# Pinv's transpositions moved into the slots, the first attn3 placed beside projections, and the first input in four parts behind products of constants

## The chip, the cores and the metric

The kernel runs on one core of a Trainium2 chip, in fp32. Its engines are TensorE (PE, with its weight loads PEld), VectorE (DVE), ScalarE (ACT), GpSimd (POOL) and SyncE (SP, which only issues DMAs here). The metric is the device time of one execution in microseconds (us). Each engine works through its own list of instructions in order; semaphores make one engine wait for another.

## The reference, cut to what matters

The input x has the shape 2 x 512 x 64 x 32: two images, 512 channels, 2048 tokens each. Two layers follow one another.

```python
# layer 0: softmax attention, 8 heads of 64
q, k = [x, emb] @ Wq, [x, emb] @ Wk ;  v = x @ Wv
x = x + softmax(q k^T / 8) v @ Wout + bout
# layer 1: Nystroem attention on LN(t), then a linear map on LN(t)
q, k, v = split(LN(t) @ Wqkv) ;  q = q * 64**-0.5
qL, kL = means of q, k over 8 tokens                 # 256 landmarks
attn1 = softmax(q kL^T) ; attn2 = softmax(qL kL^T) ; attn3 = softmax(qL k^T)
z = attn2^T / (max(col sums) * max(row sums))
for 6 iterations:  xz = attn2 z ; z = z (13 I - xz (15 I - xz (7 I - xz))) / 4
out = attn1 (z (attn3 v)) + depthwise convolution of v over 33 tokens
t = t + out @ Wout + bout
t = t + (LN(t) @ dequant(qidx, scales)^T) @ W^T
```

`pinv` below is the iteration. The scale of z contains a maximum over all images and heads, so no iteration starts before attn2 of all of them is known.

## The kernel before, in words

Channels or head dimensions lie on the 128 partitions. The eight heads of an image are worked on as four **pairs**, two heads of 64 rows in the two halves of the partitions; with two images there are eight pairs. Tokens are cut in four blocks of 512 (NTB = 4) or sixteen of 128 (NST = 16), the 512 channels in four parts of 128 (KC = 4).

**Order.** Engines PE, DVE, ACT and POOL carry out instructions in the order in which the program records them. The program is therefore a set of Python generators: each `yield` closes a unit of work, and the driving code takes units from several generators in turn, so that one's TensorE work stands between another's dependent steps. SP's queue of DMAs is ordered by the framework.

**Layer 0.** Class `Heads0` projects a pair's q, k and v; `attention0` computes scores, exponentials and products. At the start, the embedding of the frequency and time positions (`embedded`, L858 to L869) is a small product fp on TensorE, a copy ft on DVE, and an addition e_q over 128 x 2048 on POOL; `project` (L874 to L877) multiplies one 512 token block of x by a 128-column slice of Wq, and DVE adds e. The first x block is loaded by one DMA of 1 MB (L825).

**Layer 1, first part.** Class `Pair` has the parts as methods. `keys_and_queries` projects k and q and makes landmarks (L1209, label pp). `attend` makes attn2 of both heads, called X, in a tile of the single-buffered tags M0/M1 or Q0/Q1 by turns; `gram` makes the product X^T X, A; `front` is both. `others` runs the projections of an image's second to fourth pair with the front of the pair before beside them. `start_scale` forms the common scale zs from the sums of all eight pairs; its maximum over partitions is taken on POOL.

**Layer 1, main loop.** `todo` is the list of the eight pairs, the second image's first. Round n runs `pinv` for pair n. The iteration keeps, per head h, a 256 x 256 symmetric matrix and 64 more columns in the tiles M[h] and R[h]; only the upper blocks are computed, and `flip` (L1493 to L1497) supplies the lower left one: TensorE transposes a 128 x 128 block into PSUM (tp_M, tp_R), ScalarE copies it back. An iteration is: product pa of M with itself for both heads, DVE writes R and M from it (`less`, L1520); product pb of R with itself, DVE writes M. The head-0 flip of M is called before a product, the others inside one, between its first and second pass over the contraction (`between`). After the iterations three steps form u from M (wp on TensorE, a copy, tp, `less`).

Between these dependent products `pinv` calls `slot`, seventeen times a round: twice in each of five iterations, once before the last, and twice in each of the three u steps. One slot takes a unit of each of three lists: `before`, the attn1 of the previous pair (16 units: scores and exponentials twice, av with a DVE addition, row sums rs with a reciprocal and a multiplication on DVE and an addition into o on POOL, four times over); `nexts`, the `second` of the next pair (four value projections vp, nine steps of attn3, the landmark values, the convolution of v by a banded matrix, the start value y0 by the product wp_y, an ACT copy called wide, and the transposition tp_y); and, from round 5, `finish`, the output projection and last stage of the second image. In odd slots below ten a second unit of `before` follows.

The attn3 of a pair (`attn3`) has a step's scores on TensorE, the exponential p on ACT, an addition into acc3 (tags Q0/Q1) on DVE, and in the next step the product av on TensorE. The first pair has no round before it: its `second` ran beside the last pair's `front`, which takes one unit of it at its one place, and the rest then ran alone, followed by `start_scale` in between.

**The last stage.** Class `Finish1` works on a 512-token block g of the first image: the residual, then LayerNorm in steps (`statistics`: two additions on DVE, L952 and L953; mean by a product with the constant matrix mean_w on TensorE, L956; subtraction; squares; variance; root; reciprocal L1626) and the combined map of both weights (`map_units`, fp_g, L1656). The string in the driving code takes single units: 1 is attn1 of the last pair, f finish, a and b output projections of blocks 0 and 1, s a LayerNorm step of block 0.

PSUM has three sorts of banks in layer 1: `bank` (three in rotation), `product_bank` (two) and `side_bank(n)` (single ones; flips use 0, attn1's av 1, attn3's av 3).

Of the kernel before, what the change touches and what calls it, by code (L numbers as in the profile page):

```python
# [10 lines left out]
F32 = mybir.dt.float32  # L11
# [650 lines left out]
def fast_path(  # L662
# [159 lines left out]
            tiles.append(xb)  # L822
        return tiles

    xbs = load_x(x, 0, "x0", 0, 1)  # L825
    load_w0("k", slice(0, P))
    xbs += load_x(x, 0, "x0", 1, NTB - 1)
    wv_sb = wpool0.tile([P, KC, C], F32, name="wv_f")
# [349 lines left out]
    class Pair:  # L1178
# [59 lines left out]
        def attend(self):  # L1238

            i, L = self.i, self.L  # L1240
            kind = "MQ"[i % 2]
            X = self.X = [
                zpool.tile([P, 2, LM + 1], F32, tag=f"{kind}{h}", name=f"X_{i}_{h}") for h in range(2)
            ]
            rs = small.tile([P, 4], F32, tag="rs2", name=f"rs2_{i}")
            for h in range(2):
                nc.gpsimd.memset(X[h][:, :, LM:], 1.0)
            for h in range(2):
                rows_h = slice(h * D, (h + 1) * D)
                sc = bank(f"sc2_{i}_{h}")  # L1250
                for t in range(2):
                    nc.tensor.matmul(
                        sc[:, t * LM : (t + 1) * LM],
                        lhsT=L[0][rows_h, t * P : (t + 1) * P],
                        rhs=L[1][rows_h, :],
                        start=True,
                        stop=True,
                    )
                nc.scalar.activation(X[h][:, :, :LM], sc.rearrange("p (t n) -> p t n", n=LM), AF.Exp)  # L1259
            for h in range(2):  # L1260
                two = slice(2 * h, 2 * h + 2)
                x_h = X[h][:, :, :LM]
                nc.vector.tensor_reduce(rs[:, two], x_h, AX.X, ALU.add)
                nc.vector.reciprocal(rs[:, two], rs[:, two])
                nc.vector.tensor_tensor(
                    x_h, x_h, rs[:, two].unsqueeze(2).to_broadcast([P, 2, LM]), ALU.mult
                )
                nc.sync.dma_start(X_d[self.b, self.hp, h], x_h)
                nc.vector.tensor_reduce(rsum[:, i, two], x_h, AX.X, ALU.add)
# [229 lines left out]
        def pinv(self, slot):  # L1499
# [32 lines left out]
            for it in range(PINV_ITERS - 1):  # L1532
                for h in range(2):
                    pr = square(M[h], f"pa_{it}_{h}_{self.name}", flip)
                    less_in_blocks(R[h], 3.5 * CUBE, M[h], pr)
                    less_in_blocks(M[h], 3.25 / rest, M[h], pr)
                    flip = R[h], f"R{h}_{it}"
                slot()
                for h in range(2):
                    pr = square(R[h], f"pb_{it}_{h}_{self.name}", flip)  # L1540
                    less_in_blocks(M[h], rest, M[h], pr)
                    flip = None
                slot()
                self.flip(M[0], f"M0_{it}")
                flip = M[1], f"M1_{it}"
            slot()
            self.flip(*flip)

            self.u = lmpool.tile([P, 2, P], F32, tag="u", name=f"u_{self.name}")
            src = [M[h][:, :, LM:] for h in range(2)]  # L1550
# [262 lines left out]
    next(units)  # L1813
    drain(beside(pairs[0][-1].front(), units))
    drain(units)
    drain(others(1, xhs, pairs[1][0]))

    todo = pairs[1] + pairs[0]

    def second(n):  # L1820

        pair = todo[n]
        yield from pair.values(xhs_of[n // NPAIR])
        if n == NPAIR - 1:
            xhs_of.append(load_x(xh_d, 0, "xh2"))
        yield from pair.attn3()
        landmarks = pair.landmarks_values()
        next(landmarks)
        yield

        if n <= NPAIR:
            o = qopool.tile([P, S], F32, tag="qo", name=f"o_{pair.name}")
        else:
            o = None if n < len(todo) - 1 else late_buffer(f"o_{pair.name}")
        convolution = pair.convolution(o)
        next(convolution)
        yield
        next(landmarks)
        yield
        next(convolution)  # L1840
        yield
        drain(convolution)
        yield from pair.start_values()

    def late_buffer(name):

        return block_of(xpool, "xb", name).rearrange("p k n -> p (k n)")

    xhs_of = [xhs]
    todo[0].prefetch()  # L1850
    v = second(0)
    next(v)
    drain(beside(pairs[1][-1].front(), v))
    start_scale()
    drain(v)


    before, nexts, finish, made = [], [], [], 0

    def slot():  # L1860

        nonlocal made
        i = made % 17
        made += 1
        advance(before)
        advance(nexts)
        if i < 10 and i % 2:
            advance(before)
        advance(finish)

    todo[0].prefetch1(kvpool.tile([P, S], F32, tag="k", name="q2_first"))
    for n, pair in enumerate(todo):
        if n + 1 < len(todo):
            todo[n + 1].prefetch()
            nexts.append(second(n + 1))
        if n == NPAIR + 2:
# [43 lines left out]

    st = [f.steps(deviation_of(t)) for t, f in enumerate(fs)]

    for c in "1f1f1f1f11f1f1a1a1a1as1bs1s1b1b1b":
        if c == "f":
            advance(finish)
        else:
            next({"1": before[0], "a": outs[0], "b": outs[1], "s": st[0]}[c])
    assert not finish
    drain(before[0])
    drain(outs[1])  # L1930
# [12 lines left out]
    for t in range(NTB):  # L1943
        maps = fs[t].map_units(wide_banks)
        if t + 1 < NTB:
            next(st[t + 1])
            turns(maps, None, st[t + 1], None, st[t + 1], None, None, st[t + 1])
        else:
            drain(maps)
# [91 lines left out]
```

## Time and profile before

| | us |
|---|---|
| Three runs | 2883.84, 2885.5, 2886.38 |
| Median | 2885.5 |
| Profiled execution, its time | 2885.05 |
| Its span, first to last instruction | 2883.1 |
| TensorE busy | 2783.7 (97%) |
| VectorE busy | 1779.4 (62%) |
| ScalarE busy | 920.7 (32%) |
| GpSimd busy | 224.7 (8%) |
| TensorE's mean granted clock | 0.991 |
| Longest wait of PE at a flip (tp_M) | 6.0 |
| DVE reciprocal of 128 x 512, each (32 of L1599) | 3.35 |

A profile is one execution recorded by the hardware. A line of the timeline gives the start and duration in us, the engine, the line in the kernel, the operation, output and inputs by name, the shape, how many instructions are drawn together, and in brackets the idle time before it and what ended that. The waits view sums such idle time by the waiting and the releasing line: total us, times, longest. The windows view gives for a stretch each engine's busy time with the number of instructions, then the granted TensorE clock (1.00 full, 0.50 half), the DMA share and GB/s. An "issue" entry is a time in which an engine waited for nothing that the profile shows.

### The profile page before, as it was taken

The numbers are of one execution on the slowest core, as the hardware profiler recorded it, in microseconds if no ns is written. First come the engines' busy times: TensorE is split into PE (matmuls) and PEld (weight loads), VectorE is DVE, ScalarE is ACT, GpSimd is POOL, SyncE is SP. The second block draws the span as 40 slices with busy tenths as digits, with TensorE's granted clock in tenths as the row PEclk, the third lists the DMA queues.
The fourth block names the chain that finished last, engine by engine and source line by source line (L and its number), as shares of the span: only waits on it lengthen the run. The fifth ranks groups of instructions, "written<-read, shape, count | busy, mean of one in ns | idle before, by whom it ended". The sixth has DMA issues, their size and how long they took to land. (4 is left out here: it accounts for less than half of the span.)

```text
span 2883.1 us, 39570 instructions
## 1 busy us (share of the span) xinstructions
PE 2783.7 (97%) x16706; PEld 1365.1 (47%) x16706; DVE 1779.4 (62%) x2133; ACT 920.7 (32%) x1352; POOL 224.7 (8%) x130
## 2 busy tenths in 40 slices
PE   8999999999999999999999999999999999898899
PEld 4343443434443334343344456656666665554334
DVE  3869788765667766667666543464554555555565
ACT  1344434433243344344222222222322323222210
POOL 1101011010102110100011000000000000000000
PEclk9999999999999999999999999999999999999999
DMA  3000000101012000020145441102100102020201
GB/s 114 1 5 1 5 1 1 60 15 45 26 45 88 30 1 1 1 87 15 45 165 185 162 149 43 32 28 87 49 28 25 63 1 105 1 73 8 95 12 49
DMA packets 85578, 140.31 MB, mean 49 GB/s; under 512 B 7808, under 2 KB 42896, under 8 KB 82832
## 3 DMA queue, kind: packets, MB, share of 16 engines
q1 hardware_dynamic: 80896, 120.87, 12.6%
q0 software_dynamic: 4416, 16.79, 1.5%
q8 instruction: 133, 2.18, 0.3%
q14 instruction: 53, 0.43, 0.0%
q10 hardware_dynamic: 80, 0.03, 0.0%
HBM read 82.48 MB, written 55.19 MB: 48 GB/s over the span
## 5 line engine op out<-in xcount | busy, mean ns | idle before, releaser
L1053 DVE TENSOR_TENSOR acc_f<-acc_f,p_f 128x1024 f32<-128x1024 f32 x448 | 611.4, 1365 | 216.5 <-ACT p_f L1043 187.4
L1043 ACT ACTIVATE p_f<-sc_f 128x1024 f32<-128x1024 f32 x512 | 496.7, 1022 | 578.5 <-PE sc_f L1035 572.4
L1035 PE MATMUL sc_f<-q_f,k_f 64*64 64x512 f32 x4096 | 491.7, 595 | 2.9 <-ACT p_f L1043 2.9
L1065 PE MATMUL av_f<-p_f,v_f 64*64 64x512 f32 x4096 | 484.3, 589 | 0.0
L1065 PEld LDWEIGHTS av_f<-p_f,v_f 64*64 64x64 f32 x4096 | 156.5, 133 | 283.1 <-issue 283.1
L1035 PEld LDWEIGHTS sc_f<-q_f,k_f 64*64 64x64 f32 x4096 | 144.7, 133 | 293.9 <-issue 253.1
L1209 PE MATMUL pp<-xh,w 128*128 128x512 f32 x512 | 229.0, 602 | 4.2 <-ACT X L1259 3.5
L1506 PE MATMUL pa<-M 128*128 128x192 f32 (+1 forms) x640 | 157.2, 384 | 0.1
L1209 PEld LDWEIGHTS pp<-xh,w 128*128 128x128 f32 x512 | 96.5, 192 | 127.7 <-issue 115.6
L1506 PE MATMUL pb<-R 128*128 128x192 f32 (+1 forms) x640 | 152.2, 384 | 2.2 <-ACT R L1497 2.2
L1599 DVE RECIPROCAL rinv<-rinv 128x512 f32<-128x512 f32 x32 | 107.3, 3352 | 52.7 <-ACT rinv L1598 46.9
L1084 POOL TENSOR_TENSOR q_f<-q_f,rinv_f 128x512 f32<-128x512 f32 x32 | 68.3, 2135 | 825.6 <-DVE rinv_f L1083 825.5
L919 PEld LDWEIGHTS vp<-w,xh 128*128 128x128 f32 x1024 | 120.0, 196 | 21.6 <-issue 16.3
L1601 POOL TENSOR_TENSOR o<-o,rinv 128x512 f32<-128x512 f32 x32 | 46.9, 1466 | 1007.1 <-DVE rinv L1600 969.2
L919 PE MATMUL vp<-w,xh 128*128 128x128 f32 x1024 | 125.0, 282 | 0.0
L1506 PEld LDWEIGHTS pb<-R 128*128 128x128 f32 x640 | 107.3, 190 | 32.4 <-issue 10.6
L919 PEld LDWEIGHTS vp_f<-wv_f,x 128*128 128x128 f32 x1024 | 115.6, 192 | 12.7 <-issue 11.0
L1520 DVE SCALAR_TENSOR_TENSOR R<-M,pa 128x320 f32<-128x320 f32 (+1 forms) x160 | 60.0, 416 | 98.2 <-PE pa L1506 97.2
L1520 DVE SCALAR_TENSOR_TENSOR M<-M,pb 128x320 f32<-128x320 f32 (+1 forms) x160 | 59.3, 416 | 99.3 <-PE pb L1506 97.7
L874 PE MATMUL pp_q_f<-x,wq_f 128*128 128x512 f32 x256 | 118.0, 614 | 1.8 <-DVE q_f L877 0.7
L919 PE MATMUL vp_f<-wv_f,x 128*128 128x128 f32 x1024 | 118.5, 276 | 0.0
L934 PE MATMUL yp_f<-q_f,wo_f 128*128 128x512 f32 x256 | 114.2, 599 | 4.3 <-DVE rinv_f L1083 3.3
(192 smaller groups left out, 3153.8 us busy)
## 6 DMA issues: line engine op xcount, KB each, us to landing
xh<-xh_fd SPq DMA_DIRECT2D x12, 1024.0 KB, 5.1
x<-in_x_dram SPq DMA_DIRECT2D x8, 1024.0 KB, 5.3
xr_f<-in_x_dram SPq DMA_DIRECT2D x8, 1024.0 KB, 5.1
x_fd<-xr_f POOLq DMA_DIRECT2D x8, 1024.0 KB, 4.6
xh_fd<-xn_f POOLq DMA_DIRECT2D x8, 1024.0 KB, 4.6
k_fd<-k SPq DMA_DIRECT2D x32, 256.0 KB, 2.6
q_fd<-q SPq DMA_DIRECT2D x32, 256.0 KB, 2.8
xb_g<-x_fd SPq DMA_DIRECT2D x32, 256.0 KB, 4.7
```

The source lines that it names most:

```text
L874: nc.tensor.matmul(pp, lhsT=w_sb[kind][:, k, cols], rhs=xbs[t][:, k, :], start=k == 0, stop=k == KC - 1)
L919: nc.tensor.matmul(vp[:, j * P : (j + 1) * P], lhsT=xb[:, k, j * P : (j + 1) * P], rhs=w_of(k), start=k == 0, stop=k == KC - 1,)
L934: nc.tensor.matmul(yp, lhsT=wo_sb[:, k, m * P : (m + 1) * P], rhs=oTs[k][:, toks], start=k == 0, stop=k == NPAIR - 1,)
L1035: nc.tensor.matmul(sc[r * D : (r + 1) * D, h, :], lhsT=hd.k[rows, lo : lo + D], rhs=hd.q[rows, t * TB : (t + 1) * TB], start=True, stop=True,)
L1043: nc.scalar.activation(p, sc, AF.Exp, scale=D**-0.5)
L1053: nc.vector.tensor_tensor(acc, first if c == 1 else acc, p, ALU.add)
L1065: nc.tensor.matmul(av[r][half, :], lhsT=hd.v[keys, c, half], rhs=pp[keys, h, :], start=c == 0, stop=c == NST - 1,)
L1084: nc.gpsimd.tensor_tensor(o, o, rinv, ALU.mult)
L1209: nc.tensor.matmul(pp, lhsT=self.w[j][:, c, :], rhs=xhs[t][:, c, :], start=c == 0, stop=c == KC - 1)
L1506: nc.tensor.matmul(dst, lhsT=lhsT[:, k, t * P : (t + 1) * P], rhs=rhs[:, k, :], start=k == 0, stop=k == 1)
L1520: nc.vector.scalar_tensor_tensor(out, m, scale, pr, ALU.mult, ALU.subtract)
L1599: nc.vector.reciprocal(rinv, rinv)
```

## The change

- **The first input.** The DMA of the first x block is cut in four, one for each 128 channels. Twenty products of the constant mean_w with itself are put into an otherwise unused bank ahead of the first product on TensorE.
- **Tags of X.** `attend` always uses the tags M0/M1, no longer Q0/Q1 in turn.
- **Flips.** In `pinv`, the flip of R[0] leaves the inside of the product pa of head 1 and goes into the following slot; the flip of M[0] leaves its place just before the next product and goes into the slot before it; so does the last flip of M[1]. `slot` takes a function `between` for this and calls it after the first unit of `before`, ahead of `nexts`. The flips of R[1] and M[1] stay inside products.
- **Two units in slot 0.** The first slot of each round takes two units of `nexts` instead of one.
- **y0.** In `second`, the product wp_y comes before the convolution's second half, and tp_y after it; before, both came after.
- **The first pair's attn3.** `second(0)` is taken one unit at a time beside the projections of the second image's later pairs (`others(1, ...)`), from the eleventh unit on. The next pair's prefetch and value projections stand around the last pair's `front` and `start_scale`, before round 0, so round 0's slots have fewer units of `nexts` left.
- **The end.** A "t" at the end of the string takes the first LayerNorm step of block 1 (the two DVE additions) ahead of block 0's reciprocal; the loop then doesn't take it a second time.

```diff
@@ -822,7 +822,12 @@
             tiles.append(xb)
         return tiles
 
-    xbs = load_x(x, 0, "x0", 0, 1)
+    xbs = [block_of(xpool, "xb", "x0_0_0")]
+    for k in range(KC):
+        nc.sync.dma_start(xbs[0][:, k, :], chunked(x[0])[:, k, :TB])
+    warm = bank("warm")
+    for i in range(20):
+        nc.tensor.matmul(warm[:, :P], lhsT=mean_w, rhs=mean_w, start=True, stop=True)
     load_w0("k", slice(0, P))
     xbs += load_x(x, 0, "x0", 1, NTB - 1)
     wv_sb = wpool0.tile([P, KC, C], F32, name="wv_f")
@@ -1238,10 +1243,7 @@
         def attend(self):
 
             i, L = self.i, self.L
-            kind = "MQ"[i % 2]
-            X = self.X = [
-                zpool.tile([P, 2, LM + 1], F32, tag=f"{kind}{h}", name=f"X_{i}_{h}") for h in range(2)
-            ]
+            X = self.X = [zpool.tile([P, 2, LM + 1], F32, tag=f"M{h}", name=f"X_{i}_{h}") for h in range(2)]
             rs = small.tile([P, 4], F32, tag="rs2", name=f"rs2_{i}")
             for h in range(2):
                 nc.gpsimd.memset(X[h][:, :, LM:], 1.0)
@@ -1534,17 +1536,16 @@
                     pr = square(M[h], f"pa_{it}_{h}_{self.name}", flip)
                     less_in_blocks(R[h], 3.5 * CUBE, M[h], pr)
                     less_in_blocks(M[h], 3.25 / rest, M[h], pr)
-                    flip = R[h], f"R{h}_{it}"
-                slot()
+                    flip = None
+                slot(lambda: self.flip(R[0], f"R0_{it}"))
+                flip = R[1], f"R1_{it}"
                 for h in range(2):
                     pr = square(R[h], f"pb_{it}_{h}_{self.name}", flip)
                     less_in_blocks(M[h], rest, M[h], pr)
                     flip = None
-                slot()
-                self.flip(M[0], f"M0_{it}")
+                slot(lambda: self.flip(M[0], f"M0_{it}"))
                 flip = M[1], f"M1_{it}"
-            slot()
-            self.flip(*flip)
+            slot(lambda: self.flip(*flip))
 
             self.u = lmpool.tile([P, 2, P], F32, tag="u", name=f"u_{self.name}")
             src = [M[h][:, :, LM:] for h in range(2)]
@@ -1813,8 +1814,6 @@
     next(units)
     drain(beside(pairs[0][-1].front(), units))
     drain(units)
-    drain(others(1, xhs, pairs[1][0]))
-
     todo = pairs[1] + pairs[0]
 
     def second(n):
@@ -1837,40 +1836,54 @@
         yield
         next(landmarks)
         yield
+        start = pair.start_values()
+        next(start)
+        yield
         next(convolution)
         yield
         drain(convolution)
-        yield from pair.start_values()
+        next(start)
+        yield
 
     def late_buffer(name):
 
         return block_of(xpool, "xb", name).rearrange("p k n -> p (k n)")
 
+
     xhs_of = [xhs]
-    todo[0].prefetch()
-    v = second(0)
-    next(v)
-    drain(beside(pairs[1][-1].front(), v))
+    first = second(0)
+    for i, _ in enumerate(others(1, xhs, todo[0])):
+        if i == 8:
+            todo[0].prefetch()
+        if i >= 10:
+            next(first, None)
+    drain(first)
+    todo[1].prefetch()
+    nexts = [second(1)]
+    advance(nexts)
+    for n in todo[NPAIR - 1].front():
+        advance(nexts, n // 2)
     start_scale()
-    drain(v)
-
-
-    before, nexts, finish, made = [], [], [], 0
-
-    def slot():
+    advance(nexts)
+
+
+    before, finish, made = [], [], 0
+
+    def slot(between=lambda: None):
 
         nonlocal made
         i = made % 17
         made += 1
         advance(before)
-        advance(nexts)
+        between()
+        advance(nexts, 2 if i == 0 else 1)
         if i < 10 and i % 2:
             advance(before)
         advance(finish)
 
     todo[0].prefetch1(kvpool.tile([P, S], F32, tag="k", name="q2_first"))
     for n, pair in enumerate(todo):
-        if n + 1 < len(todo):
+        if n and n + 1 < len(todo):
             todo[n + 1].prefetch()
             nexts.append(second(n + 1))
         if n == NPAIR + 2:
@@ -1920,11 +1933,11 @@
 
     st = [f.steps(deviation_of(t)) for t, f in enumerate(fs)]
 
-    for c in "1f1f1f1f11f1f1a1a1a1as1bs1s1b1b1b":
+    for c in "1f1f1f1f11f1f1a1a1a1as1bs1s1b1b1bt":
         if c == "f":
             advance(finish)
         else:
-            next({"1": before[0], "a": outs[0], "b": outs[1], "s": st[0]}[c])
+            next({"1": before[0], "a": outs[0], "b": outs[1], "s": st[0], "t": st[1]}[c])
     assert not finish
     drain(before[0])
     drain(outs[1])
@@ -1943,7 +1956,8 @@
     for t in range(NTB):
         maps = fs[t].map_units(wide_banks)
         if t + 1 < NTB:
-            next(st[t + 1])
+            if t:
+                next(st[t + 1])
             turns(maps, None, st[t + 1], None, st[t + 1], None, None, st[t + 1])
         else:
             drain(maps)
```

## The prediction

> **What bounds the kernel now.** I read the page's shares of busy time first, then its chain that ended last.
>
> ```profile
> PE 2783.7 (97%) x16706; PEld 1365.1 (47%) x16706; DVE 1779.4 (62%) x2133; ACT 920.7 (32%) x1352; POOL 224.7 (8%) x130
> PE 40%; DVE 4%; ACT 1%; issue 1%; DMA 0%; POOL 0%; ACTq 0%; DVEq 0%; SPq 0%; POOLq 0%
> ```
>
> TensorE is the bound: 2883.1 - 2783.7 leaves 99 us in which it does nothing, and the change adds next to no work for it. So a gain can only come out of its waits and out of stretches at a low clock. Next, the waits of PE (total us, times, longest us):
>
> ```profile
> PE tp_R L1496 <- DVE R L1520: 17.2, 10, 4.9
> PE tp_M L1496 <- ACT M L1497: 8.2, 2, 6.0
> PE av L1351 <- ACT p L1343: 5.9, 9, 0.7
> PE rs L1381 <- DVE acc L1365: 4.7, 8, 1.0
> PE mean_g L956 <- DVE xn_g L953: 3.9, 2, 3.1
> PE tp_y L1490 <- ACT wide L1485: 3.4, 6, 0.8
> ```
>
> These rows are the transpositions (flips) of pinv, the first pair's attn3, the landmark sums, the last LayerNorm and the transposition of y0. They are what the change touches. To see how each arises I read the timeline (start, us, engine, work, idle before and its releaser). First pair's attn3, with nothing beside it:
>
> ```profile
> 1752.58 1.13 PE L1334 MATMUL sc<-L,k 64*128 64x256 f32 x8
> 1753.74 1.09 ACT L1343 ACTIVATE p<-sc 128x512 f32<-128x512 f32 x2 [2.23 <-PE sc L1334]
> 1754.39 1.57 PE L1351 MATMUL av<-p,v 128*64 128x256 f32 x8 [0.68 <-ACT p L1343]
> ```
>
> TensorE waits 0.68 us for the exponentials of each step, eight times. A pinv round:
>
> ```profile
> 1873.80 1.08 PE L1594 MATMUL rs<-acc,ones 128*64 128x512 f32 x4
> 1875.54 3.35 DVE L1599 RECIPROCAL rinv<-rinv 128x512 f32<-128x512 f32 x1 [5.39 <-ACT rinv L1598]
> 1879.61 0.74 DVE L1520 SCALAR_TENSOR_TENSOR R<-M,pa 128x320 f32<-128x320 f32 x2
> 1880.23 0.30 PE L1496 MATMUL tp_R<-ident,R 128*128 128x128 f32 x1 [2.07 <-DVE R L1520]
> ```
>
> The attn1 unit's reciprocal holds VectorE for 3.35 us and its multiplication for 0.69. R's update stands behind both, and the flip, called inside the next product, behind that: 2.07 us. The windows view (PE, PEld, DVE, ACT, POOL busy, clock) right after:
>
> ```profile
> 1880.82:1884.23 3.41, 3.41 (x10) 1.60 (x10) 1.61 (x5) 1.01 (x3) 0.30 (x1) 0.50 0.00 0
> ```
>
> TensorE busy throughout, at half clock: the wait costs a second time, 1.7 us. All half-rate stretches together last 55.6 us, 27.8 us of loss. Last, the end:
>
> ```profile
> 2782.75 3.68 PE L1656 MATMUL fp_g<-xn_g,mT 128*128 128x512 f32 x8
> 2787.48 1.23 DVE L952 TENSOR_TENSOR xn_g<-xb_g 128x1024 f32<-128x1024 f32 x1
> 2788.74 0.69 DVE L953 TENSOR_TENSOR xn_g<-xn_g 128x512 f32<-128x512 f32 x1
> 2789.49 2.08 PE L956 MATMUL mean_g<-xn_g,mean_w 128*128 128x512 f32 x2 [3.05 <-DVE xn_g L953]
> ```
>
> and the head:
>
> ```profile
> 14.91 3.62 POOL L862 TENSOR_TENSOR e_q_f<-ft_q_f 128x2048 f32<-128x2048 f32 x1 [11.50 <-issue]
> 19.32 7.13 PE L874 MATMUL pp_q_f<-x,wq_f 128*128 128x512 f32 x16 [0.72 <-DVE q_f L877]
> ```
>
> [...] here a 2.07 us wait was followed by a drop and the same wait in later rounds was not always, so I price it as a chance. [...] attn3's additions take 1.29 us a pair, 2.35 beside GpSimd's addition into o. [...] e_q's input is there at 9.62, e_q starts at 14.91.
>
> **The change, part by part.** The sum is against the profiled execution, 2885.05 us (span 2883.1, 1.9 around it); the three runs have the median 2885.5, 0.5 more.
>
> *Head: 0.* Twenty products of constants go ahead of fp_q, which waits until 8.62 for the embedding's DMA; they end some 3 us before that. One DMA of 1 MB becomes four, three more issues on SP's queue, ahead of the k weights and blocks x1 to x3 there (x lands 6.86, x1 10.8, needed later). The 16 matmuls before 13.73 ran at half rate (9.34 us instead of 7.13). Yet faster ones gain nothing: the third block's bank needs q_f's addition, which needs e_q, which ends at 18.53 whatever TensorE does. Bounds: -1.7 if e_q comes earlier with its input; +0.7 if the queue is late.
>
> *First attn3 beside projections: -4.4.* Removed: 8 x 0.68, 0.54 (tp behind the landmark addition) and 0.47 (tp_y): 6.45; and 1.14 of gaps in round 0, whose slots change. A projection block (3.43 us, the pp rows) now stands between scores and av, against 1.09 of exponentials. Round 0 loses four value units (3.77 each) to the time before it, so 14 next-pair units fill 17 slots. I estimate new gaps there: 0.68 (first two attn3 steps back to back), 0.75 and 0.9 (wp behind the M1 flip and behind an empty slot), 0.3, 0.55: 3.2. Bounds of those 0 and 6. X now always in tag M lets each attend wait on the previous gram, which ended a projection run earlier: nothing. start_scale's chain (normalisation, gram, column sums, GpSimd's reduction) ends an estimated 10 us after the last scores, and TensorE has three value units and the second gram, 13.9 us: hidden; it had some 45 us of cover, and without this one would cost up to 10 once.
>
> *Rounds 1 to 4: -1.6 each, and the clock.* Removed per round: 2.1 and 0.6 (flips of R0 behind the reciprocal), 0.21 + 0.96 (landmark sums: attn3 is one unit earlier), 0.25 (wp), 0.53 (tp_y: the convolution's second half, 2.9 us, stands between it and its copy): 4.65. What is late next: the R0 flip, now in the slot after the attn1 unit (1.05 us of scores cover it) and ahead of the attn3 step, still misses VectorE in slot 2 by 0.65; the M0 flip, formerly after the slot, now has only the attn1 unit ahead of it and stands behind slot 4's reciprocal and the slow additions: 0.9; the u steps' second wp behind reciprocal, multiplication, the landmarks' reciprocal (1.75) and yT (0.42): 1.5. New: 3.05. Each of these is bounded by 0 and by the 2.1 seen. -1.6 x 4 = -6.4. Two of the half-clock stretches, 1880.82 and 2102.69, begin with waits of 2.1 us; with none so long both go: -3.4. Together -9.8. Queued behind a flip that waits: its slot's attn3 or convolution unit and, on ScalarE, the flip's copy (0.27); the products need that copy anyway.
>
> *Rounds 5 to 7: -6.5.* Round 5's 2.2 (M flip's copy behind Finish squares) to 1.1. Round 6's 4.9 to 3.4, as half a product and an attn1 unit now stand ahead of that flip; the 2.18 at 2505 stays (R1, not moved). Round 7's 5.95 becomes about 5.0 at R0, the products start earlier, with 0.75 of clock: -2.4, and 1.47 goes: -3.9. Bounds: 0 and -14.5, the whole of these waits.
>
> *End: -6.1.* The two part additions of the second last-stage block (1.23 + 0.69) stood behind the first block's reciprocal, 3.34 us; now they come ahead of it. The mean can start when the matmuls end, 2786.43, not 2789.49: 3.06. The half-clock stretch 2788.76 to 2795.59 follows that wait; without it 6.83 us of work take 3.4: about 3.05. If the reciprocal becomes late by the same 1.9 us, the first map's output waits for it: TensorE has 3.68 us of fp_g queued, so nothing.
>
> Sum: 0 - 4.4 - 9.8 - 6.5 - 6.1 = -26.8: 2858.
>
> **Rivals.** (1) *The waits only move.* VectorE's pile (reciprocal, multiplication, updates, 4.8 us in a row) stays the length it was, and the flips meet it elsewhere. For: the same instructions in nearly the same order on VectorE; TensorE can't wait less than the pile unless more work stands ahead. Against: the attn1 scores do stand ahead. Then only the first attn3 (4.4), tp_y (4 x 0.6 = 2.4) and the end (6.1) count: -13, 2872. (2) *All of it goes.* Waits of 17.2 + 8.2 + 4.7 + 2.9 + 5.9 + 3.1 = 42 and about 11.5 of clock, less 2: -51.5, 2834. For: nothing else is on those lines; against: the 4.9 and 6.0 waits have ScalarE's squares ahead of them, which are not moved. (3) *Slower: the moved flips starve the slots.* R0 and M0 flips now stop TensorE ahead of the attn3 unit, which before was the work that filled this very time. If in slots 2 and 5 of each round each waits 2.1 us and drops the clock for one 3.41 us stretch (1.7), and the u chain waits 1.5, a round has 9.1 (2 x 3.8 + 1.5) against 5.75 before (4.65, 0.85 of clock as the mean of rounds 1 to 4, and 0.25 for scores behind ScalarE): +3.4 x 7 = +24; less attn3 and end, 10.5: +13, 2898. It decides once a round's loss passes 5.75 + 10.5/7 = 7.2 us. For: the M0 flip loses a next-pair unit of about 2 us as cover; against: in slot 5 a 1.08 us unit and VectorE's order (updates ahead of the attn3 additions) are left. (4) *It doesn't do what it says*: [...] attn3's gaps reopen in round 0, the flips move: within 6 us of 2885.
>
> **How the numbers follow.** Likeliest, 2846 to 2868: 0.58. Rival 1: 0.15. Rival 2: 0.11. Rival 3: 0.10. Rival 4: 0.06. A measurement of this kernel tells 0.2%, 5.8 us, from no change. Faster 0.84, same 0.06, slower 0.10. The range 2840 to 2877 holds the first two cases and, from 2840 up, the near half of the second rival, 0.79.
>
> **What would show it.** Right: between 1734 and 1770 no PE wait for p; tp_R's row down from 17.2 to about 10 with none over 2.2 before round 5; the row of rs <- acc near 0; mean_g's 3.05 gone; half-clock total near 35 us. New rows for tp_R and tp_M under slots 2 and 5, below 1 us each. Wrong if those pass 2 us, if the first tile of round 0 waits for zs, or if the list of half-rate stretches grows. The head is right if fp_q, e_q and the third block start at 8.6, 14.9 and 19.3 as before.

## The result, and the profile after

The changed kernel takes 2863.76 us (median of six runs, 2859.83 to 2866.89) against 2885.34 (six runs, 2882.31 to 2886.92). The ratio is 0.9925, 95% interval 0.9912 to 0.9938: 21.6 us faster. The forecast was 2858. The profiled execution of the changed kernel is the slowest of the six, 2866.89 with a span of 2865.2; against the 2883.1 of before that is 17.9 less.

The page of the changed kernel, first lines of the engines and of the chain that ended last:

```profile
PE 2789.3 (97%) x16746; PEld 1365.6 (48%) x16746; DVE 1773.2 (62%) x2133; ACT 917.1 (32%) x1352; POOL 223.6 (8%) x130
PE 39%; DVE 4%; ACT 1%; issue 1%; DMA 0%; POOL 0%; DVEq 0%; ACTq 0%; SPq 0%; POOLq 0%
```

TensorE is still the bound, with 76 us of idle time where there were 99. Its waits now (total us, times, longest us):

```profile
PE wp L1483 <- DVE R L1522: 12.5, 8, 2.4
PE tp_R L1498 <- DVE R L1522: 6.0, 6, 3.2
PE tp_M L1498 <- DVE M L1522: 4.9, 7, 2.2
PE pa L1508 <- ACT M L1499: 4.2, 1, 4.2
PE pp_q_f L879 <- DVE q_f L882: 3.9, 1, 3.9
PE av L1353 <- ACT p L1345: 0.7, 1, 0.7
PE mean_g L961 <- DVE xn_g L958: 0.9, 1, 0.9
```

tp_R went from 17.2 to 6.0, av from 5.9 to 0.7, the last 3.1 of mean_g is gone. Three rows are new or grown: wp, tp_M behind VectorE, and the head's pp_q_f (0.7 before). Of the kernel before:

```profile
PE wp L1481 <- DVE R L1520: 4.4, 7, 2.4
PE tp_M L1496 <- DVE M L1470: 0.8, 1, 0.8
```

I cut both traces at the same pieces of work: the first exponential of layer 0, its last, and the first transposition of M in each round. A half-rate stretch is a time in which the granted clock was 0.50. One of 3.41 us makes a round 1.65 us longer, as the experiments show, about half its length. So the column "at full clock" is an estimate: from each duration, half of its half-rate time is taken off, before and after. Duration of each stretch, in us:

| Stretch | before | after | difference | forecast | difference at full clock |
|---|---|---|---|---|---|
| head | 56.6 | 58.8 | +2.2 | 0 | +0.5 |
| layer 0 | 1351.6 | 1352.8 | +1.2 | 0 | -0.5 |
| projections, first attn3, round 0 | 447.6 | 439.8 | -7.9 | -4.4 | -7.9 |
| rounds 1 to 4 | 442.3 | 431.5 | -10.8 | -9.8 | -9.1 |
| round 5 | 146.6 | 148.2 | +1.7 | -1.1 | +1.7 |
| round 6 | 149.7 | 150.5 | +0.8 | -1.5 | +2.5 |
| round 7 and end | 288.7 | 283.6 | -5.1 | -10.0 | -5.1 |
| sum | 2883.1 | 2865.2 | -17.9 | -26.8 | -18.0 |

Layer 0, which the change leaves alone, has two half-rate stretches where it had one; that is its +1.2. In all, the half-rate time is the same in both executions, 53.4 and 53.5 us.

**Rounds 1 to 4.** The timeline of the changed kernel at the place shown before:

```profile
1874.66 3.35 DVE L1600 RECIPROCAL rinv<-rinv 128x512 f32<-128x512 f32 x1 [5.45 <-ACT rinv L1599]
1877.69 1.13 PE L1575 MATMUL sc<-q_first,L 64*128 64x512 f32 x4
1878.72 0.74 DVE L1522 SCALAR_TENSOR_TENSOR R<-M,pa 128x320 f32<-128x320 f32 x2
1879.26 0.33 PE L1498 MATMUL tp_R<-ident,R 128*128 128x128 f32 x1 [0.44 <-DVE R L1522]
```

VectorE's pile is as long as it was, reciprocal, multiplication, R's update. But 1.13 us of attn1 scores and the second half of a product now stand ahead of the flip, so it waits 0.44, not 2.07. What is late next is the second wp of the u steps, in each of the four rounds:

```profile
1940.00 3.35 DVE L1600 RECIPROCAL rinv<-rinv 128x512 f32<-128x512 f32 x1
1943.45 0.69 DVE L1601 TENSOR_TENSOR rinv<-av,rinv 128x512 f32<-128x512 f32 x1
1944.06 1.74 DVE L1393 RECIPROCAL acc<-acc 128x256 f32<-128x256 f32 x1
1945.90 0.42 DVE L1394 TENSOR_TENSOR acc<-av,acc 128x256 f32<-128x256 f32 x1
1946.25 0.47 DVE L1522 SCALAR_TENSOR_TENSOR R<-M,tp 128x128 f32<-128x128 f32 x2
1946.67 1.18 PE L1483 MATMUL wp<-M,R 128*64 128x256 f32 x8 [1.64 <-DVE R L1522]
```

**Rounds 5 to 7.** Here VectorE and ScalarE also carry the last stage of the other image. Round 5, the flip of M0, moved ahead of its slot's attn3 step:

```profile
2344.30 2.35 DVE L1367 TENSOR_TENSOR acc<-acc,p 128x512 f32<-128x512 f32 x2
2346.58 1.21 DVE L957 TENSOR_TENSOR xn_g<-xb_g 128x1024 f32<-128x1024 f32 x1
2347.82 0.69 DVE L958 TENSOR_TENSOR xn_g<-xn_g 128x512 f32<-128x512 f32 x1
2348.43 1.41 DVE L1522 SCALAR_TENSOR_TENSOR M<-M,pb 128x320 f32<-128x320 f32 x4
2348.97 0.33 PE L1498 MATMUL tp_M<-ident,M 128*128 128x128 f32 x1 [2.17 <-DVE M L1522]
```

M's update stands behind slow additions (2.35 us for the pair, with GpSimd's addition into o beside it from 2344.53 to 2346.11; pairs with none beside them take 1.29) and the LayerNorm's two: a wait of 2.17 replaces the old 2.21. So the waits of this round are as long as before (TensorE's idle time is 2.6 and 2.7 us), and its extra 1.7 us lie in TensorE's busy time. In round 6 a residual whose block is still on its way stands ahead of R's update:

```profile
2561.74 0.75 DVE L946 SCALAR_TENSOR_TENSOR xb_g<-yp_g,b_f,xb_g 128x512 f32<-128x512 f32 x1 [7.23 <-DMA xb_g<-x_fd]
2562.41 0.48 DVE L1522 SCALAR_TENSOR_TENSOR R<-M,tp 128x128 f32<-128x128 f32 x2
2562.83 2.07 PE L1483 MATMUL wp<-M,R 128*64 128x256 f32 x8 [2.40 <-DVE R L1522]
```

In round 7 a flip's copy on ScalarE stands behind a square that waits for a buffer, which GpSimd frees:

```profile
2602.19 0.63 ACT L968 ACTIVATE sq_g<-xn_g 128x512 f32<-128x512 f32 x1 [4.46 <-POOL o L1602]
2602.73 0.25 ACT L1499 COPY M<-tp_M 128x128 f32<-128x128 f32 x1
2603.03 1.05 PE L1508 MATMUL pa<-M 128*128 128x320 f32 x2 [4.16 <-ACT M L1499]
```

**End.** The part additions come ahead of the reciprocal, and the mean follows fp_g at once:

```profile
2773.27 0.69 DVE L958 TENSOR_TENSOR xn_g<-xn_g 128x512 f32<-128x512 f32 x1
2773.88 3.34 DVE L1627 RECIPROCAL rstd_g<-rstd_g 128x512 f32<-128x512 f32 x1
2774.02 1.13 PE L961 MATMUL mean_g<-xn_g,mean_w 128*128 128x512 f32 x2
```

**Head.** The first 16 products take 7.35 us instead of 9.34 and are done 2.4 us sooner, and TensorE then waits 3.9 us for e_q instead of 0.7. The windows view (last columns: granted clock, DMA share, GB/s) shows what follows:

```profile
15.70 3.62 POOL L867 TENSOR_TENSOR e_q_f<-ft_q_f 128x2048 f32<-128x2048 f32 x1 [12.29 <-issue]
20.10 4.25 PE L879 MATMUL pp_q_f<-x,wq_f 128*128 128x512 f32 x6 [3.91 <-DVE q_f L882]
19.57:22.98 3.41, 2.88 (x4) 1.32 (x5) 1.07 (x2) 0.00 (x0) 0.00 (x0) 0.50 1.08 319
```

### The profile page after: what moved, and what is told of

The parts are those of the page before. It is cut to its first block, busy times and chain, and to the rows that moved or that the text cites. A ratio compares the mean times of both kernels' runs of the same rounds, so it can differ in the third digit from the quotient of the medians.

```text
span 2865.2 us, 39650 instructions
## 1 busy us (share of the span) xinstructions
PE 2789.3 (97%) x16746; PEld 1365.6 (48%) x16746; DVE 1773.2 (62%) x2133; ACT 917.1 (32%) x1352; POOL 223.6 (8%) x130
## 5 line engine op out<-in xcount | busy, mean ns | idle before, releaser
L1600 DVE RECIPROCAL rinv<-rinv 128x512 f32<-128x512 f32 x32 | 107.2, 3351 | 53.0 <-ACT rinv L1599 47.5
L1508 PEld LDWEIGHTS pa<-M 128*128 128x128 f32 x640 | 108.0, 192 | 44.6 <-issue 10.5
L1508 PEld LDWEIGHTS pb<-R 128*128 128x128 f32 x640 | 108.6, 192 | 33.0 <-issue 10.9
L1367 DVE TENSOR_TENSOR acc<-acc,p 128x512 f32<-128x512 f32 x96 | 74.8, 821 | 73.1 <-ACT p L1345 73.1
L924 PE MATMUL vp<-w,xh 128*128 128x128 f32 x1024 | 119.2, 276 | 0.0
L939 PE MATMUL yp_g<-o,wo_f 128*128 128x512 f32 x256 | 117.7, 607 | 1.4 <-ACT p L1580 1.1
```

The source lines that it names most:

```text
L924: nc.tensor.matmul(vp[:, j * P : (j + 1) * P], lhsT=xb[:, k, j * P : (j + 1) * P], rhs=w_of(k), start=k == 0, stop=k == KC - 1,)
L939: nc.tensor.matmul(yp, lhsT=wo_sb[:, k, m * P : (m + 1) * P], rhs=oTs[k][:, toks], start=k == 0, stop=k == NPAIR - 1,)
L1367: nc.vector.tensor_tensor(self.acc3[h], src, p[:, h, :], ALU.add)
L1508: nc.tensor.matmul(dst, lhsT=lhsT[:, k, t * P : (t + 1) * P], rhs=rhs[:, k, :], start=k == 0, stop=k == 1)
L1600: nc.vector.reciprocal(rinv, rinv)
```

## The experiments

My theory of the result: the flips gain mostly by staying clear of the halved clock; the first attn3 and the end gain their waits; the head loses a little. Rivals: the waits only move, the head is free, single parts are worth nothing. Each ratio is to runs of the kernel before on the same chip; the intervals are about 0.0013 each way, 3.7 us. Where a run is called slower by so many us, two medians are compared that may come from different chips; taken from the ratios, the figures differ by up to 2 us (11.5 instead of 9.9 for the flips). So I read small effects from the durations of stretches, with and without a half-rate stretch in them. Such a stretch costs a round 1.65 us: round 3 of the changed kernel takes 108.81 with one and 107.17 without, in two executions. The tags of X were not undone alone: what they are worth is not shown. TensorE's waits for X in the projections are 3.9 us, where they were 3.5.

**The changed kernel again** (same kernel, another execution):

> The changed kernel itself once more, beside the next two. Theory: the waits of TensorE are the same within 0.5 us in all, the half-rate stretches fall elsewhere, because windows of 3.41 us lie differently to the program in each execution; the median stays within 3 us of 2863.8 and the single times spread by about 7 us.

Measured 2864.90 (2859.89 to 2870.07), ratio 0.9925 again. TensorE's idle time is 76.5 us against 75.9, but half-rate time 60.6 against 53.5; the profiled span is 2868.4 against 2865.2. The kernel does the same and the clock makes the difference.

With the half-rate time taken off, round 1 lasts 107.0 to 107.2 us in the six executions that have it in this order, two of them with a half-rate stretch in it: so the estimate holds there. It can be used on executions without a trace too, since the span and the mean granted clock of each were measured. Span times clock estimates what an execution would last at full clock, and the rest is what half clock took. The clock is known to 0.001, 2.9 us, so a mean over five or six runs is good to about 1 us. The means, in us:

| Kernel | runs | at full clock | taken by half clock |
|---|---|---|---|
| before, on four chips | 11 to 15 each | 2854.6 to 2855.0 | 26.7 to 28.6 |
| changed, first and again | 6, 6 | 2837.9, 2837.4 | 23.9, 25.8 |
| flips back | 6 | 2839.7 | 32.1 |
| the end's step back | 6 | 2840.7 | 29.2 |
| first attn3 back | 6 | 2844.3 | 25.4 |
| y0 back | 4 | 2840.5 | 28.0 |
| one unit in slot 0 | 6 | 2841.7 | 23.4 |
| the head undone | 5 | 2837.8 | 24.6 |
| products of constants out | 5 | 2837.8 | 24.6 |
| landmark unit later | 8 | 2838.7 | 33.8 |
| three mends | 5 | 2835.9 | 29.8 |
| attn1 ahead, with and without the products | 5, 5 | 2841.0, 2840.3 | 24.6, 24.1 |

The change takes 17.2 us out at full clock, and about 3 more by less half-rate time. Its parts, undone one at a time, come to 18.5 at full clock (flips 2.0, end 3.0, first attn3 6.6, y0 2.8, slot 0 4.0, head 0.1), which is the whole within what these means can tell.

All half-rate stretches of one execution start on one grid of 3.413 us, which lies differently to the kernel each time: in the profiled executions of before and of the changed kernel its step is 3.4133 us, and the stretches start 0.08 and 2.50 us past a multiple of that. I laid that grid over the 14 traces of this study and summed TensorE's idle time in each of its windows at full clock. Idle of 2.0 us or more: 105 windows, all followed by half clock. 1.6 to 2.0: 20 of 67. 1.0 to 1.6: 24 of 133. Under 1.0: none of 11188. So in this kernel a wait of 2 us that falls in one window costs 1.65 us more, nearly as much again.

**Flips back.**

```diff
-                    flip = None
-                slot(lambda: self.flip(R[0], f"R0_{it}"))
-                flip = R[1], f"R1_{it}"
+                    flip = R[h], f"R{h}_{it}"
+                slot()
...
-                slot(lambda: self.flip(M[0], f"M0_{it}"))
+                slot()
+                self.flip(M[0], f"M0_{it}")
...
-            slot(lambda: self.flip(*flip))
+            slot()
+            self.flip(*flip)
```

> The changed kernel with pinv's transpositions back at their old places, all else kept. Theory: moving them took about 1.9 us of idle time out of each of rounds 1 to 4 (2.1 + 0.6 became 0.4 to 0.85 + 0.3) and 1.7 to 1.8 out of each of rounds 6 and 7: this kernel is 8 to 13 us slower than the changed one, 2872 to 2877, with tp_R's row of waits back near 17. Rival (the waits only move): within 2 us of the changed kernel.

Measured 2873.68, ratio 0.9965 (0.9951 to 0.9978): 9.9 us slower than the changed kernel, as the theory said. Its waits, and the three windows after the waits in rounds 1, 2 and 3 (the clock is the third column from the end):

```profile
PE tp_R L1498 <- DVE R L1522: 17.1, 10, 4.9
PE wp L1483 <- DVE R L1522: 10.6, 8, 2.4
```

```profile
1880.61:1884.02 3.41, 3.41 (x8) 1.17 (x6) 1.82 (x6) 0.80 (x3) 0.51 (x1) 0.50 0.00 0
1989.83:1993.24 3.41, 3.41 (x9) 1.27 (x7) 1.94 (x6) 0.60 (x2) 0.62 (x1) 0.50 0.00 0
2099.06:2102.47 3.41, 3.41 (x8) 1.51 (x9) 2.18 (x7) 0.27 (x1) 0.86 (x1) 0.50 0.01 2
```

The waits of 2.06 to 2.12 fell inside a window three times of four. Rounds 1 to 4 last 109.29, 109.47, 109.69 and 108.71; with 1.65 taken off the first three they are 107.6, 107.8, 108.0 and 108.7. The changed kernel without half clock has 107.10, 107.50, 107.17 and 108.07. So the flips are worth 0.3 to 0.9 us a round in themselves, 2.4 for four, and 1.65 more in each round where the clock falls. That 2.4 is less than the idle time says, which is 5.9 us more here in the four rounds (16.8 against 10.9). Round 7 and end have 4.2 us more idle time (25.5 against 21.2), of which 1.5 shows in their duration at full clock. In round 5 the moved flips are worth less than nothing: at full clock it lasts 147.4 to 148.2 in six executions with the flips moved and 145.8 here; how they lengthen it is not shown. Over all runs the flips are worth 2 us at full clock and about 7 of clock (32.1 against 23.9 and 25.8): the theory's main point holds.

**The end's step back.**

```diff
-    for c in "1f1f1f1f11f1f1a1a1a1as1bs1s1b1b1bt":
+    for c in "1f1f1f1f11f1f1a1a1a1as1bs1s1b1b1b":
...
-            if t:
-                next(st[t + 1])
+            next(st[t + 1])
```

> The changed kernel without the early first step of the second last-stage block: the two part additions again behind the first block's reciprocal. Forecast's step: 6.1 us slower (3.05 of wait and 3.05 of clock), 2870. Rival: only the wait, [...]: 3 us, 2867. Rival 2: nothing, if the additions only push the reciprocal: 2864.

Measured 2870.82, ratio 0.9955 (0.9940 to 0.9970): 7.1 slower. The wait is back, its longest 3.1, with a half-rate stretch from 2779.86 right behind it.

```profile
PE mean_g L961 <- DVE xn_g L958: 3.9, 2, 3.1
```

In the traces round 7 and end are 287.2 against 283.6, 3.6 apart. 3.05 of it is the wait; how much clock comes with it depends on what else falls in that execution. Over all runs it is 3.0 us at full clock and about 4 of clock, so the forecast's step of 6.1 holds on the average, with both its halves.

**First attn3 back.**

```diff
-    first = second(0)
-    for i, _ in enumerate(others(1, xhs, todo[0])):
...
-    todo[1].prefetch()
-    nexts = [second(1)]
...
+    drain(others(1, xhs, todo[0]))
+    todo[0].prefetch()
+    v = second(0)
+    next(v)
+    drain(beside(pairs[1][-1].front(), v))
+    start_scale()
+    drain(v)
+    nexts = []
...
-        if n and n + 1 < len(todo):
+        if n + 1 < len(todo):
```

> The changed kernel with the first pair's values and attn3 as before: one value unit beside the last pair's front, the rest alone; all else as changed. Between the two traces the stretch from the projections to the end of round 0 is 7.9 us shorter. Theory: nearly all of that is this part, since the eight waits of 0.68 at av, 0.54 and 0.47 come back and round 0 has its 18 next-pair units again: slower than the changed kernel by 7 to 9, near 2872. The forecast's step: 4.4, near 2868. Rival: the gain of that stretch belongs to the flips and slots of round 0, then the difference is under 2.

Measured 2870.56, ratio 0.9953 (0.9941 to 0.9965): 6.8 slower.

```profile
PE av L1353 <- ACT p L1345: 5.9, 9, 0.7
```

Projections to round 0 last 446.6 against 439.8 to 440.4. 5.4 of the 6.2 to 6.9 is idle time. Over all runs it is 6.6 us at full clock and next to nothing of clock. The stretch belongs to this part, not to the flips; 1.0 us of its 7.9 does not (446.6 here, 447.6 before).

**y0 back.**

```diff
-        start = pair.start_values()
-        next(start)
-        yield
         next(convolution)
         yield
         drain(convolution)
-        next(start)
-        yield
+        yield from pair.start_values()
```

> The changed kernel with y0's product and transposition again both behind the convolution. Forecast's step: tp_y waits 0.5 to 0.85 for the copy in seven rounds, 3.4 to 4 us slower, near 2867.5. Rival: the late product of the u steps (wp) then waits as much less, and the time is unchanged.

Measured 2869.94 in four runs (2866.72 to 2875.23), ratio 0.9943 (0.9929 to 0.9958). Its rounds don't say so: with 1.65 off where the clock fell, rounds 1 to 4 last 107.3, 107.7, 107.4 and 107.6, 0.1 us more in all than the changed kernel. tp_y waits 0.16 and wp 1.64, as in the changed kernel. What the profiled execution has is 67 us of half rate, 14 more. So in rounds 1 to 4 the order of y0 is worth next to nothing with two units in slot 0, though not for the rival's reason, as wp waits no less. Over the four runs 3 us are of clock and 2.8 are left at full clock, a difference that four runs barely show (the trace has 1.3); whether they are y0's stays open.

**One unit in slot 0.**

```diff
-        advance(nexts, 2 if i == 0 else 1)
+        advance(nexts)
```

> The changed kernel with one unit of the next pair in slot 0 again, so that each later unit of a round stands one slot later. Theory: in rounds 1 to 4 the waits only change places: 0.21 + 0.96 come back at the landmark sums and 1.64 at wp goes down to about 0.25, 0.2 a round less; in round 6 the wait of 2.4 us at wp, where VectorE has a residual ahead of R's update whose block is still on its way, goes: near 2861. Rival, from the run with the landmark unit one slot later: the wait moves to the landmarks' transposition and passes 2 us, which brings the half clock with it each time: 4 x 2, near 2872.

Measured 2867.45, ratio 0.9942: 3.7 slower, between theory and rival; at full clock 4.0, with no more half-rate time. The landmark sums wait 0.80 and 0.96 in each round (row below), the products around them run thinner, and rounds 1 to 4 last 108.81, 109.21, 108.87 and 109.27 with no half clock: 6.3 more in all. That is far more than the idle time says, which grows by 0.6: wp waits 0.25 a round now and the rest is in the busy time. Round 0 is 1.6 shorter, and round 6's wait of 2.4 behind the load is gone (147.5 instead of 150.5 with one half-rate stretch less).

```profile
PE rs L1383 <- DVE acc L1367: 7.0, 8, 1.0
```

**The head undone, and the products alone taken out** (the second has the last three lines of this edit only).

```diff
-    xbs = [block_of(xpool, "xb", "x0_0_0")]
-    for k in range(KC):
-        nc.sync.dma_start(xbs[0][:, k, :], chunked(x[0])[:, k, :TB])
+    xbs = load_x(x, 0, "x0", 0, 1)
-    warm = bank("warm")
-    for i in range(20):
-        nc.tensor.matmul(warm[:, :P], lhsT=mean_w, rhs=mean_w, start=True, stop=True)
```

> The changed kernel with its first part undone: the first x block again in one DMA, no products of constants. Theory: the head costs the changed kernel about 2.2 us, because the faster first 16 products only lengthen TensorE's wait for e_q's addition (3.9 us instead of 0.7) and the clock is halved after that wait. Expected: e_q starts at 14.9 again, the third block at 19.3 after a wait of 0.7, no half-rate stretch at 19.6, the first exponential 2.2 us earlier; median near 2861.5. Rival, the forecast's own step: the head is free, so the median stays at 2863.8 within 1.

> The changed kernel without the twenty products of constants, the x block still in four DMAs. If the products cost (idle and clock), the first 16 products run at half rate again and end at about 18.6, the wait for e_q is about 1.5 us, no half-rate stretch follows and what is left is only a later e_q: 0.8 us of cost, median near 2862.4. If the four DMAs are the cost, e_q starts at 15.7; if they have no part in it, e_q starts at 14.9 and the run equals the one with the whole head undone.

Medians 2863.76 and 2864.78: no difference that these runs can show. The traces show one. In the five executions without the products the head lasts 56.0 to 57.2, mean 56.6, and no half-rate stretch follows its wait for e_q; in the nine with them 55.8 to 60.1, mean 58.0, and such a stretch follows in six. e_q starts at 14.7 and 14.9 in the two executions with one DMA and between 14.1 and 15.7 in those with four, so the four DMAs show no clear effect on it. The products of constants cost 1.4 us on average, all of it by the clock: with half of the half-rate time taken off, the head lasts 56.5 with them and 56.6 without. The time that they save goes into a longer wait for e_q: it is 2.78 to 3.94 us in the six executions with a stretch behind it, 1.19, 1.92 and 2.90 in the three others with the products, and at most 2.09 in the five without.

**The landmark unit one slot later.**

```diff
         landmarks = pair.landmarks_values()
-        next(landmarks)
-        yield
...
         next(convolution)
         yield
         next(landmarks)
         yield
+        next(landmarks)
+        yield
```

> The changed kernel with the first landmark unit moved behind the first half of the convolution (one unit later), so that VectorE updates R for the second wp before the landmarks' reciprocal. Theory: the wait of 1.64 us at wp in rounds 1 to 4 is the reciprocal (1.74) and yT (0.42) ahead of R's update. It goes, about 0.6 comes at the landmarks' transposition: 4 x 1.0 less, near 2859.5. Rival: the whole wait moves to that transposition, no gain. In rounds 5 and 6 no change.

Measured 2874.60, ratio 0.9963 (0.9952 to 0.9974): 10.8 slower, the rival and more. wp no longer waits, but the unit's sums now come later too, and with them the reciprocal. The timeline:

```profile
1944.11 0.48 DVE L1522 SCALAR_TENSOR_TENSOR R<-M,tp 128x128 f32<-128x128 f32 x2
1945.56 1.75 DVE L1393 RECIPROCAL acc<-acc 128x256 f32<-128x256 f32 x1 [0.97 <-ACT acc L1392]
1947.99 0.41 PE L1402 MATMUL tp<-ident,acc 128*128 128x128 f32 x2 [2.04 <-DVE acc L1394]
```

The wait grew by only 0.4, from 1.64 to 2.04 (3.03 in round 4), but that puts it over 2.0, and the clock fell in all four rounds of this execution: stretches from 1948.85, 2058.08, 2167.30 and 2276.53. The first and last windows:

```profile
1948.85:1952.26 3.41, 3.40 (x16) 1.95 (x18) 0.29 (x2) 0.37 (x1) 0.00 (x0) 0.50 0.18 58
2276.53:2279.94 3.41, 3.17 (x18) 1.73 (x18) 0.49 (x2) 0.67 (x2) 0.00 (x0) 0.50 0.23 62
```

Over the eight runs the loss is 1 us at full clock and 9 of clock.

**Three mends at once**: no products of constants, the landmark unit later, and one row of squares in the deviation's buffer. It contains the edit of the run before, and so its fault. The edit's third part:

```diff
-                return sq, *(row_of(f"sq{k}_{self.name}").unsqueeze(1) for k in (2, 3))
+                return sq, *(row(f"sq{k}_{self.name}").unsqueeze(1) for k, row in ((2, deviation), (3, row_of)))
```

> The changed kernel with three mends: no products of constants at the head, the landmark unit one later as in the run before, and the squares of the last stage in another buffer, so that ScalarE's square doesn't wait for GpSimd's addition with a flip's copy behind it. Theory: 2.4 at the head, 4 at wp, and of the waits of 4.16 and 1.77 us for flips' copies about 4: near 2853.5. Rival: the last-stage waits only move to VectorE's additions of the squares, then near 2857.5.

Measured 2867.65, ratio 0.9940. ScalarE's square no longer waits for GpSimd and the 4.16 is gone; in its place the flip of R0 waits 3.43 for VectorE in the same round, where the squares' additions stand. The row of tp_R is 9.5 now. Most of the wait moved. Yet at full clock this kernel is 1.8 us shorter than the changed one, and its round 7 and end 268.5 against 269.8 and 270.5; half clock takes 5 us more.

**The attn1 of the previous pair one unit ahead from slot 8**, with and without the products of constants.

```diff
-        if i < 10 and i % 2:
+        if i in (1, 3, 5, 7, 8, 9):
```

> The changed kernel with the previous pair's attn1 one unit ahead from slot 8 on (slot 8 takes two units), so that its last reciprocal (3.35 us) is over when the u steps begin. Theory: the wait of 1.64 us at wp in rounds 1 to 4 is the pile of that reciprocal, its multiplication and the landmarks' reciprocal; it falls to about 0.3: 4 x 1.3 less, and 1 to 2 us of clock, near 2857. Rival: the landmark sums wait for the last attn3 addition instead, which now stands behind the reciprocal, by 1 us or more a round: no gain.

> As the run before, without the products of constants at the head. Theory: the head is 1 to 2.4 us shorter when a clock drop after the wait for e_q goes away: near 2855.5. Rival: the start of e_q, which differs by over 1 us between executions, hides it: equal to the run before.

Measured 2868.41 (0.9942) and 2866.93 (0.9937), against 2864.90 of the changed kernel beside them: by themselves within the intervals, but at full clock both are longer, by 3.6 and 2.8 us. The first run's rival holds: the 1.64 went down to 0.17, and the landmark sums wait 0.96 for the last attn3 addition, the last av 0.42.

```profile
PE rs L1383 <- DVE acc L1367: 3.8, 4, 1.0
```

The profile's idle time of rounds 1 to 4 is no larger, 10.4 against 11.0, yet they last 434.8 without a half-rate stretch, 5 us more than the changed kernel's 429.8. In round 2 the busy time of rs is 6.01 us against 5.35, of av 16.90 against 16.42, of wp 3.67 against 3.25, for as many matmuls. Why they take longer is not shown. Without the products of constants nothing clear changes, as that run's rival said.

## Why the prediction was right, and where not

The size and sign came true: forecast -26.8, measured -21.6 by medians and -17.9 in the profiled execution; 2863.76 lies in the likeliest case's own range, 2846 to 2868. The working is less good than the sum. At full clock the forecast is -19.6 and the two executions differ by -18.0, but this comes of errors that cancel, which is luck: the first attn3 and rounds 1 to 4 gave 6.2 us more than forecast, rounds 5 to 7 and the end 7.9 less.

- **First attn3**: forecast -4.4, measured -7.9, and 6.8 by undoing it. Right mechanism: the waits for the exponentials are gone. The term that was mis-sized is the new gaps of round 0, put at 3.2 in place of 1.14: round 0 has 1.7 us of idle time, 0.5 more than before. Idle time in all fell by 5.5; what makes up the rest of the 7.9 is not shown.
- **Rounds 1 to 4**: -9.8 forecast, -10.8 measured. The three waits named as late next are there: R0 0.44 to 0.85 (forecast 0.65), M0 0.31 (0.9), wp 1.64 (1.5). That "both half-clock stretches go" was right for two, but wp brought one back in round 3. The sum is right, but not its parts. At full clock, undoing them one at a time costs these rounds 2.4 (flips), 6.3 (the second unit in slot 0) and 0.1 (y0), together 8.8 of the 9.1. The forecast had 4.6 for the flips (2.7 a round less the new 1.55), nothing for the second unit (1.17 and 0.25 less the new 1.5) and 2.1 for y0. It counted idle time, and most of what the second unit gains is not idle time.
- **Rounds 5 to 7 failed**: -6.5 forecast. The step assumed that a flip with more TensorE work ahead of it waits that much less. In round 5 M0's flip lost a next-pair unit as cover while VectorE had the attn3 and LayerNorm additions ahead of M's update: 2.17 for 2.21. That takes the gain away; the 1.7 us of loss is busy time that came with the moved flips, and its cause stays open. In round 6 the 4.9 fell to 3.25 as said (3.4), but M0 (1.27) and the residual behind its load (2.40) came new. Round 7 kept most of what was forecast, 4.16 instead of 5.95 and no 1.47, less 0.75 more at its start (1.59 for 0.84); of the 2.4 that was forecast for the 5.95, the terms given make only 1.7 (0.95 and 0.75). This is rival 1, the waits only move, confined to the rounds in which VectorE carries a third kind of work.
- **End**: the 3.05 of wait is right. The 3.05 of clock isn't a fixed sum: in the profiled execution another window fell instead (2753.6), while over the runs with and without the step it comes to about 4.
- **Head**: "0" was wrong by its own argument. It said that faster products gain nothing because e_q gates; it didn't follow the wait so made, nor the clock behind it. The bound of +0.7 counted only a late queue. Nor does e_q follow its input at a fixed distance: it starts 3.9 to 6.5 us after it in the 14 executions, and the 5.3 us of before (9.62 to 14.91) are one case among them.
- **The clock** as a sum of stretches seen in one execution was the wrong term: I took 7.2 us of gain from it, and the two profiled executions have the same half-rate time, 53.4 and 53.5. Over all runs the clock gives about 3 us. A stretch seen once is a draw. The grid starts at 0.08 us in the one and at 2.50 in the other, so the same wait is cut differently by it: wp's 1.64 us of rounds 1 to 4 lie in windows with 1.64, 1.36, 1.78 and 1.63 us of idle time, and of these the third alone has half clock behind it.
- **The signs** named beforehand: of those for being right, tp_R's row went to 6.0 (about 10 was forecast), rs <- acc and mean_g's 3.05 are gone, and no flip waits over 2.2 before round 5. But half-rate time did not go to 35 us, the list of its stretches grew from 10 to 13, and e_q and the third block start at 15.7 and 20.1 instead of 14.9 and 19.3. The first two speak against the clock term, the last against the head.
- Rival 3, flips that starve the slots, would have needed over 2 us in slots 2 and 5 of each round; those of rounds 1 to 4 show 0.3 to 0.85.

## What to carry to other kernels

Price a wait of the bounding engine with the clock that goes with it: here 2 us of idle time in one window of the 3.413 us grid cost 1.65 us more, and 1.6 us mostly nothing (20 of the 67 windows with 1.6 to 2.0 us had a drop behind them). Waits of 2.04 to 2.12 us in rounds 1 to 4 brought a drop in 9 of 14 cases, those of 1.64 in 6 of 28; so by an estimate from these counts, the half microsecond from 2.1 to 1.6 is worth 1.2 us, and each further one little more than its own length. Judge edits by the time at full clock and by the half-rate time apart, over several runs: idle time alone missed most of what the second unit in slot 0 gained. When work is moved ahead of a dependent step, list the other engine's queue behind it for each kind of round; a forecast from a round with two kinds of work doesn't hold where a third joins. And here, twenty products ahead of an addition that they don't move only lengthened the wait for it, from 0.7 to 3.9 us.

## What was not expected of the hardware

- The drop follows idle time per window with a sharp edge: 105 of 105 windows with 2.0 us or more, none of 11188 under 1.0, and a mixed zone between them. In that zone the drops at 1.0 to 1.4 us lie at two kinds of places only, the projections' start (1518 to 1562) and the attn1 scores of the end (2706 to 2758), where 64-row score products make up most of the busy part (1.9 of 2.3 us in the changed kernel's window from 1521.4).
- The same kernel spreads over 7 to 10 us, mostly for this reason (2859.8 to 2866.9, 2859.9 to 2870.1), more than several of the edits are worth.
- TensorE's busy time grew by over 5 us in four rounds with the same products in another order (attn1 ahead). The idle time there showed nothing of it (10.4 us against 11.0); the duration of a stretch is the safer measure.
